# A four-layer network on one core: two of its statistics by accumulating ScalarE instructions, and a gate's factor by TensorE

## The chip, the core and the metric

The kernel runs on one core of a Trainium2 chip. A core has five engines with a queue each: TensorE (PE; its weight loads are listed apart as PEld), VectorE (DVE), ScalarE (ACT), GpSimd (POOL) and SyncE (SP, which here only issues DMAs). TensorE writes to PSUM alone, which has eight banks of 128 x 512 float32; VectorE and ScalarE read and write both PSUM and the working memory SBUF. The metric is the time of one execution in microseconds (us); the kernel is executed several times and the median is given.

## What is computed

The input is 16 images of 64 x 64 tokens with 256 channels, float32. There are four layers, each `x = x + layer(gn(x))`, where `gn` normalizes an image over 32 groups of 8 channels: the mean and the variance of a group are taken over all 4096 tokens and 8 channels.

```python
x = x + L0(gn(x))   # nearest of 1024 code vectors for each token
x = x + L1(gn(x))   # sigmoid attention along each image row
x = x + L2(gn(x))   # gate * gn(x), one gate per token
x = x + L3(gn(x))   # linear attention with 4 heads, then a layer norm
```

So four sets of statistics are needed per image: of the input, of layer 0's output, of layer 1's output and of layer 2's output. In layer 2 the gate of token n is a sigmoid of a softmax-weighted sum over all 4096 tokens. With gn(x) = (x - mean) * scale, and a mean that a later normalization takes out again, the output of layer 2 can be written per channel as (x - mean) * (1 + gate * scale); the kernel does that.

## The kernel before

The image is worked on with channels on the partitions: 256 channels are two blocks (index k) of 128, and 4096 tokens are 8 chunks (index ch) of 512. A chunk is a tile of 128 x 2 x 512 float32, 512 KB. Each layer is a Python generator per image that emits instructions for some chunks and then yields; a heap at the end of the program (`tasks`, `queue`, lines 891 to 921) interleaves the generators of different images by virtual start times and lengths (`LAG1`, `LEN1` and so on), in units of one image's search. In the steady state the search of image b (layer 0, `stage1`) is interleaved with layer 1 of image b-1 and the exponentials, the gate and layer 3 of earlier images. A scheduler then fixes one order per engine at compile time, by priority and by when it expects operands to be ready; `tc.high_priority` moves an instruction forward. On the chip each engine takes its queue in that order, and semaphores hold an instruction until its operands are there.

What the change touches:

- `chunk_stats` (line 255) issues one `bn_stats` on VectorE per chunk and block, which gives count, mean and variance of 512 elements. `gn_finish` (line 259) merges the eight chunks with `bn_aggr` and turns the per-channel numbers into `scale` and `-mean` per group, with small matmuls, ScalarE and GpSimd instructions.
- `back` (line 357, in `stage1`) finishes layer 0 for a chunk: TensorE transposes the tokens (input row plus code vector, added by a gathering DMA) to channels on partitions, into a PSUM bank `pt`; ScalarE copies `pt` to SBUF (line 364); VectorE takes statistics of that copy (line 257, tile `st_s<-xt_s`); the copy is stored.
- `stage2` (line 603) makes the exponentials (line 628, ScalarE) and their weighted sums (line 631, VectorE), and from them the gates, which it transposes to rows, copies and stores to memory as float32 (lines 649 to 652).
- `gate2` (line 664) loads a chunk of layer 1's output (`xg`), loads its 512 gates copied to all 128 partitions (`gb`, 256 KB written), and for each block: ScalarE makes `u = 1 + gate * scale` (line 685), VectorE makes `xg = (xg - mean) * u` (line 686) and takes statistics of it (line 257, tile `st_g<-xg_g`). The chunk goes to `out`, where layer 3 reads it.

PSUM is split into a pool of four banks (`ps_m`, the function `bank`), which nearly all stages share, and one of two double banks (`ps_w`, `wide`) for the search, `ph` and `po`. `put_row` (line 143) is the pattern that the change's new helper follows: a float32 row is cut into three bfloat16 parts whose sum gives it to about float32 precision, and a bfloat16 matmul against ones puts their sum on all partitions.

Of the kernel before, what the change touches and what calls it, by code (L numbers as in the profile page):

```python
# [16 lines left out]
P = 128  # L17
# [24 lines left out]
def kernel(  # L42
# [70 lines left out]
    PARTS = 3  # L113
    ones3 = const.tile([P, P], BF16, name="ones3")
# [5 lines left out]
    for n in range(PARTS - 1):  # L120
        nc.vector.tensor_scalar(
            below[:, n, n + 1 :], ident[0:PARTS, n + 1 : PARTS], -1.0, None, ALU.mult
        )

# [134 lines left out]
    def gn_finish(st, kind, b):  # L259

        tag = f"{kind}_{b}"
        mv = small.tile([P, NK, 2], F32, tag="gn_mv", name=f"mv_{tag}")
        for k in range(NK):
            nc.vector.bn_aggr(mv[:, k, :], st[:, k, :, :].rearrange("p c s -> p (c s)"))
        mean = mv[:, :, 0]
# [30 lines left out]
    def stats0(b):  # L296
# [8 lines left out]
        with tc.high_priority(offset=URGENT):  # L305
            norm0[b] = gn_finish(st, "n0", b)
# [5 lines left out]
    def stage1(b):  # L312
        tag = f"s1_{b}"
        scale, _, nbias = norm0.pop(b)
# [39 lines left out]
        st1 = stats_tile(1, f"st1_{tag}")  # L354
        x1_d[b] = []

        def back(ch):
            for k in range(NK):
# [5 lines left out]
                nc.scalar.copy(xt[ch][:, k, :], pt)  # L364
            chunk_stats(st1, xt[ch], ch)
# [51 lines left out]
        with tc.high_priority(offset=URGENT):  # L417
            norm1[b] = gn_finish(st1, "n1", b)
# [5 lines left out]
    def layer1(b):  # L424
# [118 lines left out]
        with tc.high_priority(offset=URGENT):  # L543
            norm2[b] = gn_finish(st2, "n2", b)
# [58 lines left out]
    def stage2(b, parts=1):  # L603
# [15 lines left out]
        gd = dram.tile([NT, P], F32, tag="gate", name=f"gd_{tag}")  # L619
        gates_d[b] = gd  # L620
        yield 2
        rest = gate2(b) if parts > 1 else None
        for part in range(parts):
# [26 lines left out]
            grow = small.tile([NT, P], F32, tag="grow", name=f"grow_{tag}_{part}", bufs=1)  # L650
            nc.scalar.copy(grow[:n, :], pg[:n, :P])
            nc.scalar.dma_start(out=gd[cols, :], in_=grow[:n, :])
# [11 lines left out]
    def gate2(b):  # L664
        tag = f"g2_{b}"
        scale, nmean, _ = norm2.pop(b)
        gd, x2 = gates_d.pop(b), x2_d.pop(b)
        st3 = stats_tile(3, f"st3_{tag}")
# [5 lines left out]
        for ch in range(NCHUNK):  # L674
            xt = xg.tile([P, NK, CW], F32, tag="xg", name=f"xg_{tag}_{ch}")
            nc.sync.dma_start(out=xt, in_=x2[ch])
            gb = s3p.tile([P, CW], F32, tag="gb", name=f"gb_{tag}_{ch}", bufs=2)
            nc.sync.dma_start(
                out=gb,
                in_=gd[ch * CH : (ch + 1) * CH, :].rearrange("t p -> (t p)").rearrange("(o n) -> o n", o=1)  # L680
                .to_broadcast([P, CW]),
            )
            for k in range(NK):
                u = s3p.tile([P, CW], F32, tag="u2", name=f"u_{tag}_{ch}_{k}")
                nc.scalar.activation(u, gb, AF.Identity, bias=one, scale=scale[:, k : k + 1])
                nc.vector.scalar_tensor_tensor(  # L686
                    xt[:, k, :], xt[:, k, :], nmean[:, k : k + 1], u, op0=ALU.add, op1=ALU.mult
                )
            chunk_stats(st3, xt, ch)
# [269 lines left out]
```

## Time and profile before

| | |
|---|---|
| median of 3 runs | 5701.88 us (5696.69 to 5706.75) |
| profiled execution | 5709.26 us; its span, first to last instruction, 5707.6 us |
| mean granted TensorE clock | 0.941 |
| busy: PE, DVE, ACT, POOL | 5070.7, 5046.3, 4578.7, 1929.1 us |
| `bn_stats` on DVE, line 257 | 4 x 256 instructions, 167.5 + 165.0 + 164.7 + 163.4 us |
| `u` on ACT, line 685 | 256 instructions, 199.4 us |
| copy of `pt` on ACT, line 364 | 256 instructions, 137.3 us |

In the groups of instructions a row gives line, engine, operation, the tiles out<-in, the shapes, the count; then busy time and mean duration of one; then the idle time of that engine just before them and what ended it. In the waits a row gives who waited for whom, the total, how often, and the longest. Durations of neighbours on an engine can overlap by some tens of nanoseconds, so that what one more instruction costs is better read from the distance between starts in the timeline.

### The profile page before, as it was taken

The page shows a single profiled execution, that of the slowest core. Times are in us where ns is not written, and L with a number is a line of the kernel's source. Part 1 is how long each engine was busy: PE and PEld are TensorE (multiplying, and loading weights), DVE is VectorE, ACT ScalarE, POOL GpSimd, SP SyncE. Part 2 cuts the span into 40 slices and gives each one's busy share as a digit, 9 for nine tenths or more (in the row PEclk, how much of TensorE's full clock was granted, in tenths as well). Part 3 has the DMA queues.
Part 4 walks back from the last instruction along what each step waited for, and adds up shares of the span by engine and source line. Part 5 has one row for each costly group of instructions (what it writes and reads, how often), then busy time and mean ns, then how long its engine had stood idle before and what let it go on. Part 6 is the DMA issues. An engine that isn't in the chain of part 4 may idle for free.

```text
span 5707.6 us, 71918 instructions
## 1 busy us (share of the span) xinstructions
PE 5070.7 (89%) x24911; PEld 2999.1 (53%) x24911; DVE 5046.3 (88%) x7186; ACT 4578.7 (80%) x6578; POOL 1929.1 (34%) x1203
## 2 busy tenths in 40 slices
PE   8978899889999999999989999899999999997777
PEld 3534455445555565554645555564555545564444
DVE  6489798999999999998999999999898998988982
ACT  4478587978889798887978888798887878888873
POOL 3123233323333334334333333333333333321332
PEclk9988999989999999999999999999999999997888
DMA  6453835655666757566575756757475674745544
GB/s 187 141 158 93 265 112 188 176 161 177 191 188 176 212 160 198 175 190 186 170 205 163 187 188 177 203 161 218 143 193 172 184 207 142 203 153 160 158 137 92
DMA packets 453763, 991.87 MB, mean 174 GB/s; under 512 B 50456, under 2 KB 198808, under 8 KB 445208
## 3 DMA queue, kind: packets, MB, share of 16 engines
q1 hardware_dynamic: 320272, 750.88, 39.7%
q0 software_dynamic: 92160, 134.26, 15.5%
q10 hardware_dynamic: 40968, 102.13, 4.6%
q8 instruction: 198, 3.24, 0.2%
q14 instruction: 165, 1.35, 0.1%
HBM read 684.07 MB, written 303.04 MB: 173 GB/s over the span
## 4 chain that ended last, share of the span: by engine, by line
PE 34%; DVE 19%; ACT 13%; issue 6%; POOL 3%; DMA 3%; ACTq 0%; SPq 0%; POOLq 0%; DVEq 0%
PE pd_s L386 11%; DVE ex_s L631 7%; ACT ex_s L628 6%; PE ph_l L476 3%; DVE i_s L397 3%; PE pqv_s L762 2%; PE pxo_s L874 2%; PE pk_s L745 2%; ACT nn_s L381 2%; DVE nn_s L392 2%; POOL qv_s L780 1%; PE po_l L516 1%; PE pz_s L835 1%; DVE st_s L257 1%; DVE xg_g L686 1%
## 5 line engine op out<-in xcount | busy, mean ns | idle before, releaser
L631 DVE CUSTOM_DVE_ANT_0 ex_s<-ex_s,x2b 128x2048 f32<-128x2048 f32 x1024 | 2364.2, 2315 | 77.0 <-ACT ex_s L628 75.1
L628 ACT ACTIVATE ex_s<-x0b,nmax_s,x_r 128x2048 f32<-128x2048 f32 x1024 | 2137.9, 2088 | 80.8 <-DVE num_s L631 77.8
L386 PE MATMUL pd_s<-e,xn_s 128*128 128x512 f32 x4096 | 2008.5, 625 | 71.6 <-DVE m L392 61.5
L398 POOL DMA_INDIRECT xc_s<-in_emb_rows,i_s x512 | 1160.6, 2267 | 1794.2 <-DVE i_s L397 1255.3
L386 PEld LDWEIGHTS pd_s<-e,xn_s 128*128 128x128 f32 x4096 | 763.4, 198 | 855.4 <-issue 705.3
L392 DVE CUSTOM_DVE_ANT_0 nn_s<-pd_s,nn_s 128x1024 f32<-128x1024 f32 x512 | 619.7, 1213 | 137.4 <-PE pd_s L386 100.5
L381 ACT ACTIVATE nn_s<-ne,nx_s 128x1024 f32<-128x1024 f32 x512 | 580.4, 1143 | 55.9 <-DVE nx_s L352 27.5
L397 DVE FIND_INDEX8 i_s<-m,nn_s 128x8 uint32<-128x1024 f32 x512 | 623.5, 1219 | 0.0
L476 PE MATMUL ph_l<-wh_l,xt_l 128*128 128x256 f32 x2048 | 536.1, 399 | 68.0 <-DVE xt_l L521 42.6
L762 PE MATMUL pqv_s<-wqv_s,xk_s 128*128 128x256 f32 x2048 | 488.7, 380 | 0.0
L476 PEld LDWEIGHTS ph_l<-wh_l,xt_l 128*128 128x128 f32 x2048 | 386.6, 196 | 193.1 <-issue 65.9
L762 PEld LDWEIGHTS pqv_s<-wqv_s,xk_s 128*128 128x128 f32 x2048 | 388.7, 191 | 120.2 <-issue 59.8
L780 POOL TENSOR_TENSOR qv_s<-qv_s,qm_s 128x512 f32<-128x512 f32 x128 | 216.1, 1688 | 640.0 <-DVE qm_s L779 329.3
L874 PE MATMUL pxo_s<-qo_s,wctx_s 128*128 128x512 f32 x512 | 279.5, 630 | 18.5 <-DVE qo_s L854 18.1
L736 POOL TENSOR_TENSOR qv_s<-qv_s,qd_s 128x512 f32<-128x512 f32 x128 | 186.1, 1454 | 324.7 <-DVE qd_s L735 189.8
L516 PE MATMUL po_l<-blk,h_l 128*128 128x128 f32 x2048 | 286.1, 291 | 3.6 <-DVE m L392 2.9
L516 PEld LDWEIGHTS po_l<-blk,h_l 128*128 128x128 f32 x2048 | 263.1, 202 | 42.2 <-issue 22.8
L884 POOL DMA_DIRECT2D out<-y_s x128 | 118.9, 929 | 479.3 <-ACT lrs_s L845 235.2
L745 PE MATMUL pk_s<-xk_s,wk_s 128*128 128x512 f32 x512 | 259.0, 626 | 0.0
L846 POOL TENSOR_TENSOR lrs_s<-lrs_s,mhalf 128x4 f32<-128x4 f32 x128 | 199.0, 1555 | 173.1 <-ACT lrs_s L845 164.2
L361 PE MATMUL pt_s<-ident,xc_s 128*128 128x128 f32 x1024 | 157.6, 289 | 103.6 <-DMA xc_s<-in_emb_rows,i_s 70.0
L875 ACT ACTIVATE y_s<-pxo_s,xm_g 128x512 f32<-128x512 f32 x256 | 174.6, 683 | 91.3 <-PE pxo_s L874 90.6
(191 smaller groups left out, 7012.6 us busy)
## 6 DMA issues: line engine op xcount, KB each, us to landing
xs_s<-in_xT SPq DMA_DIRECT2D x128, 512.0 KB
xt_s<-in_xT SPq DMA_DIRECT2D x128, 512.0 KB
xc_s<-in_x SPq DMA_DIRECT2D x128, 512.0 KB
x_s<-xt_s ACTq DMA_DIRECT2D x128, 512.0 KB
xt_l<-x_s SPq DMA_DIRECT2D x128, 512.0 KB
x_l<-xt_l SPq DMA_DIRECT2D x128, 512.0 KB
xr_r<-x_l SPq DMA_DIRECT2D x128, 512.0 KB
xg_g<-x_l SPq DMA_DIRECT2D x128, 512.0 KB
```

The lines of the kernel that those rows point to most:

```text
L381: nc.scalar.activation(nn, ne2, AF.Identity, bias=nx2[ch][:, t : t + 1])
L386: nc.tensor.matmul(pd[:, cols], lhsT=xn[ch][:, k, t * P : (t + 1) * P], rhs=e2[:, k, cols], start=(k == 0), stop=(k == NK - 1),)
L392: nc.vector.tensor_tensor_reduce(out=nn, in0=pd, in1=nn, scale=1.0, scalar=-3.0e38, op0=ALU.add, op1=ALU.max, accum_out=m8[:, 0:1],)
L397: nc.vector.max_index(i8, m8, nn)
L398: nc.gpsimd.indirect_dma_start(out=xc[ch][:, t, :], out_offset=None, in_=emb_rows, in_offset=bass.IndirectOffsetOnAxis(ap=i8[:, 0:1], axis=0),
L476: nc.tensor.matmul(ph[:, t, :], lhsT=X[:, k, t * P : (t + 1) * P], rhs=wh_n[:, k, :], start=(t % 2 == 0 and k == 0), stop=False, skip_grou ...
L516: nc.tensor.matmul(po[:, m : m + P], lhsT=h[:, t, k * P : (k + 1) * P], rhs=at[:, t, :, :].rearrange("p r i -> p (r i)"), start=True, stop ...
L628: nc.scalar.activation(ex, x0b, AF.Exp, bias=nmax[:, T : T + 1], scale=x01[:, T, 1:2], accum_out=den[:, h, T : T + 1])
L631: nc.vector.tensor_tensor_reduce(out=ex, in0=ex, in1=x2b, scale=1.0, scalar=0.0, op0=ALU.mult, op1=ALU.add, accum_out=num[:, h, T : T + 1],)
L745: nc.tensor.matmul(pk, lhsT=wk_n[:, k, :], rhs=xt[:, k, :], start=(k == 0), stop=(k == NK - 1))
L762: nc.tensor.matmul(pqv[:, j, :], lhsT=xt[:, k, t * P : (t + 1) * P], rhs=wqv_n[:, k, :], start=(j == 0 and k == 0), stop=False, skip_group ...
L874: nc.tensor.matmul(px, lhsT=wctx[:, 1, pr * P : (pr + 1) * P], rhs=qT, start=True, stop=True)
```

## The change

Statistics of layer 0's output: the copies of line 364 become `activation(Copy)` with an accumulator output (the sum over 512 tokens), and a second ScalarE instruction squares `pt` in place, shifted by the group mean of the input, with an accumulator (the sum of squares). `bn_stats` on these chunks is gone.

The gated residual: the gates are stored as three bfloat16 parts. A chunk's gates are loaded to 3 x 3 partitions by three DMAs in place of one that filled 128. The scale is cut into three bfloat16 parts once per image by `put_scale`. One bfloat16 matmul per block of 9 products plus a row of ones gives `u` in a PSUM bank. VectorE's product reads `u` there and has an accumulator; ScalarE squares the result into the same bank with an accumulator. `bn_stats` on these chunks is gone too. `aggregate_sums` turns the sums of both places into mean and variance per channel.

```diff
+    def put_scale(dst, scale, tag):
+        v = small.tile([P, NK, GP + 1], F32, tag="v10", name=f"v10_{tag}", bufs=1)
+        nc.gpsimd.memset(v, 0.0)
+        nc.scalar.copy(v[:, :, 0:GP], scale.unsqueeze(2).to_broadcast([P, NK, GP]))
+        pb = bank(f"psr_{tag}")
+        row = pb[: GP + 1, :C]
+        for k in range(NK):
+            nc.tensor.matmul(row[:, k * P : (k + 1) * P], lhsT=v[:, k, :], rhs=ident, ...)
+        for n in range(PARTS - 1):
+            top = small.tile([GP + 1, C], BF16, tag="stop", name=f"stop_{tag}_{n}", bufs=1)
+            nc.scalar.copy(top, row)
+            nc.tensor.matmul(row, lhsT=below_s[:, n, :], rhs=top, start=False, stop=True, ...)
+        nc.scalar.activation(dst[0 : GP + 1, :], row, AF.Identity, bias=ident[0 : GP + 1, GP : GP + 1])
...
+    def aggregate_sums(st, shift, tag):
+        mv = small.tile([P, NK, 2], F32, tag="gn_mv", name=f"mv_{tag}")
+        nc.vector.tensor_reduce(mv, st.rearrange("p c k s -> p k s c"), AX.X, ALU.add)
+        nc.vector.tensor_scalar(mv, mv, 1.0 / TOK, None, ALU.mult)
+        dev = small.tile([P, NK], F32, tag="gn_dev", name=f"dev_{tag}", bufs=1)
+        if shift is None:
+            nc.vector.tensor_tensor(dev, mv[:, :, 0], mv[:, :, 0], ALU.mult)
+        else:
+            nc.vector.tensor_tensor(dev, mv[:, :, 0], shift, ALU.add)
+            nc.vector.tensor_tensor(dev, dev, dev, ALU.mult)
+        nc.vector.tensor_tensor(mv[:, :, 1], mv[:, :, 1], dev, ALU.subtract)
+        return mv
...
-                nc.scalar.copy(xt[ch][:, k, :], pt)
-            chunk_stats(st1, xt[ch], ch)
+                nc.scalar.activation(xt[ch][:, k, :], pt, AF.Copy, accum_out=st1[:, ch, k, 0:1])
+                nc.scalar.activation(
+                    pt, pt, AF.Square, bias=shift[:, k : k + 1], accum_out=st1[:, ch, k, 1:2]
+                )
...
-            norm1[b] = gn_finish(st1, "n1", b)
+            norm1[b] = gn_finish(aggregate_sums(st1, shift, f"n1_{b}"), "n1", b)
...
-        gd = dram.tile([NT, P], F32, tag="gate", name=f"gd_{tag}")
+        gd = dram.tile([PARTS, NT, P], BF16, tag="gate", name=f"gd_{tag}")
         gates_d[b] = gd
+        put_scale(scale_rows[b % 2], norm2[b][0], tag)
...
-            nc.scalar.copy(grow[:n, :], pg[:n, :P])
-            nc.scalar.dma_start(out=gd[cols, :], in_=grow[:n, :])
+            nc.scalar.copy(grow[:n, 0, :], pg[:n, :P])
+            nc.vector.tensor_tensor(left[:n, :], pg[:n, :P], grow[:n, 0, :], ALU.subtract)
+            nc.vector.tensor_copy(grow[:n, 1, :], left[:n, :])
+            nc.vector.tensor_tensor(grow[:n, 2, :], left[:n, :], grow[:n, 1, :], ALU.subtract)
+            nc.scalar.dma_start(out=gd[:, cols, :].rearrange("i t p -> t i p"), in_=grow[:n, :, :])
...
-            gb = s3p.tile([P, CW], F32, tag="gb", name=f"gb_{tag}_{ch}", bufs=2)
-            nc.sync.dma_start(out=gb, in_=gd[ch * CH : (ch + 1) * CH, :]...to_broadcast([P, CW]))
+            gr = gate_rows[ch % 2]
+            for i in range(PARTS):
+                nc.sync.dma_start(
+                    out=gr[PARTS * i : PARTS * (i + 1), :],
+                    in_=gd[i : i + 1, ch * CH : (ch + 1) * CH, :]...to_broadcast([PARTS, CW]),
+                )
             for k in range(NK):
-                u = s3p.tile([P, CW], F32, tag="u2", name=f"u_{tag}_{ch}_{k}")
-                nc.scalar.activation(u, gb, AF.Identity, bias=one, scale=scale[:, k : k + 1])
+                u = bank(f"pu_{tag}_{ch}_{k}")
+                nc.tensor.matmul(u, lhsT=srow[:, k * P : (k + 1) * P], rhs=gr, start=True, stop=True)
                 nc.vector.scalar_tensor_tensor(
-                    xt[:, k, :], xt[:, k, :], nmean[:, k : k + 1], u, op0=ALU.add, op1=ALU.mult
-                )
-            chunk_stats(st3, xt, ch)
+                    xt[:, k, :], xt[:, k, :], nmean[:, k : k + 1], u, op0=ALU.add, op1=ALU.mult,
+                    accum_out=st3[:, ch, k, 0:1],
+                )
+                nc.scalar.activation(u, xt[:, k, :], AF.Square, accum_out=st3[:, ch, k, 1:2])
...
-            scale, nmean, _ = gn_finish(st3, "n3", b)
+            scale, nmean, _ = gn_finish(aggregate_sums(st3, None, f"n3_{b}"), "n3", b)
```

The statistics of the input and of layer 1's output stay with `bn_stats` and `bn_aggr`, which `aggregate` now holds. `gate_rows` and `scale_rows` are constant tiles of 128 partitions, two of each, whose rows past the tenth stay zero.

## Prediction

> **What bounds the kernel now.** First the page's totals, then a stretch of seven images in the steady state (from the start of image 6's search to that of image 13's), since filling and draining have other limits.
>
> ```profile
> PE 5070.7 (89%) x24911; PEld 2999.1 (53%) x24911; DVE 5046.3 (88%) x7186; ACT 4578.7 (80%) x6578; POOL 1929.1 (34%) x1203
> ```
> ```profile
> core 0: us, PE busy (x) PEld busy (x) DVE busy (x) ACT busy (x) POOL busy (x), PEclk, DMA share, GB/s
> 2011.00:4361.00 2350.00, 2157.06 (x10844) 1287.70 (x10843) 2182.65 (x3104) 1988.68 (x2858) 863.08 (x517) 0.96 0.64 184
> 0.00:1017.00 1017.00, 882.47 (x4113) 475.65 (x4114) 806.92 (x1194) 693.01 (x959) 304.42 (x195) 0.93 0.55 164
> 5036.00:5708.00 672.00, 513.43 (x2402) 338.70 (x2402) 506.40 (x708) 488.11 (x756) 165.81 (x137) 0.86 0.49 139
> ```
>
> Divided by seven, one image takes 335.7 us: VectorE busy 311.8 (idle 23.9), ScalarE 284.1 (idle 51.6), TensorE 308.1. The last is flattering: matmul durations overlap. Counting from start to next start, with each interval capped at its line's median, I get 266 us of TensorE per image. So VectorE is nearest to full, with ScalarE 28 us behind. The chain that ended last agrees that no engine rules alone (PE 34%, DVE 19%, ACT 13% of the span): the three hand work to each other in fixed orders, and waits at the hand-overs make up the rest. The waits of the same seven images:
>
> ```profile
> ACT qv_s L781 <- POOL qv_s L780: 85.6, 45, 6.7
> ACT ex_s L628 <- DVE num_s L631: 44.1, 25, 2.7
> DVE ex_s L631 <- ACT ex_s L628: 37.7, 23, 3.9
> PE pt_s L361 <- ACT qv_s L767: 12.9, 7, 1.9
> ACT al_s L752 <- DVE nkm_s L751: 11.3, 9, 2.3
> ```
>
> ScalarE waits for VectorE's exponential sums 6.3 us per image, for GpSimd 12.2, the rest for many small matmul results; VectorE waits for ScalarE's exponentials 5.4.
>
> **Prices.** Groups over the whole run, then the timeline of ScalarE and of VectorE, for what one more instruction really takes.
>
> ```profile
> L257 DVE BATCH_NORM_STATS2 st_g<-xg_g 128x6 f32<-128x512 f32 x256 | 165.0, 681 | 0.1
> L257 DVE BATCH_NORM_STATS2 st_s<-xt_s 128x6 f32<-128x512 f32 x256 | 164.7, 682 | 21.0 <-ACT xt_s L364 20.9
> L875 ACT ACTIVATE y_s<-pxo_s,xm_g 128x512 f32<-128x512 f32 x256 | 174.6, 683 | 91.3 <-PE pxo_s L874 90.6
> L781 ACT ACTIVATE qv_s<-qv_s 128x512 f32<-128x512 f32 x128 | 80.5, 629 | 174.2 <-POOL qv_s L780 173.6
> ```
> ```profile
> 3405.67 0.67 ACT L754 ACTIVATE kx_s<-pk_s,nkm_s 128x512 f32<-128x512 f32 x1
> 3406.24 0.19 ACT L754 ACTIVATION_READ_ACCUMULATOR kx_s<-pk_s,nkm_s 128x1 f32 x1
> 3406.33 1.51 ACT L685 ACTIVATE u_g<-gb_g,one,s_n 128x512 f32<-128x512 f32 x2
> 3407.74 2.09 ACT L628 ACTIVATE ex_s<-x0b,nmax_s,x_r 128x2048 f32<-128x2048 f32 x1
> ```
> ```profile
> 3411.49 1.28 DVE L257 BATCH_NORM_STATS2 st_g<-xg_g 128x6 f32<-128x512 f32 x2
> 3412.69 2.28 DVE L631 CUSTOM_DVE_ANT_0 ex_s<-ex_s,x2b 128x2048 f32<-128x2048 f32 x1
> ```
>
> Start to start, a `bn_stats` takes 0.60 (1.20 for two); a PSUM activation with a pointer bias 0.57; the accumulator's read 0.09, though its row says 0.19; one `u` 0.70.
>
> **VectorE, per image.** Removed: 32 `bn_stats` x 0.60 = 19.2, and four `bn_aggr` (row mean 0.33, 0.23 start to start) = 0.9. Added: accumulator reads on 16 products, 16 x 0.08 (row of `num_s`) = 1.3; `u` now from PSUM: the nearest rows are the products with a PSUM operand, 0.341 at 128 and 0.480 at 256 elements, so by their slope about 0.76 at 512 against a median of 0.75 now: 0, between -1 (the mean now is 0.81) and +1; nine tiny operations of `aggregate_sums` about 0.1 each = 0.9; three for the gate's parts = 0.4. Net **-17.5**: 311.8 becomes 294.
>
> **ScalarE, per image.** Layer 0: 16 squares (0.57 + 0.09) = 10.6, 16 reads behind the copies = 1.5. Gate: 16 x `u` at 0.70 gives way to 16 squares without pointers, nearest L781, 0.63 less the 0.10 of overlap = 0.53, plus 0.09: -1.3. `put_scale`: a copy at 0.09 and three casts at 0.25 (starts of `put_row`'s) = 0.9. Net **+11.7**: 284.1 becomes 296. The page "ScalarE: Activation LUTs" of the Trainium skill (Rules for kernel authors) speaks against this: adds and multiplies belong on VectorE, which it calls up to three times as fast per element, for bfloat16. Here data is float32 and the rows give 0.66 against 0.60, so moving a statistic costs a tenth, not threefold; by the rule's factor ScalarE would gain 29 us instead of 12 and the change would lose about 15 per image. I take the rows.
>
> **TensorE.** 16 bfloat16 matmuls of 512 columns; the nearest, L481, has a row of 0.388 but 0.215 start to start: 3.4, and 0.5 for `put_scale`. 266 becomes 270; hidden in its idle 66. Without that cover, 3.9.
>
> **DMAs.** 128 gate loads of 256 KB become 384 of 3 KB: 33 MB of 992 less to move, and nothing now waits for that bandwidth (64% busy). SP issues two more per chunk, 0.32 each (its row at the end of the run); loads queued behind them come 0.64 later, and they have two to four buffers: 0, or 5 us per image if not. GpSimd gets one memset per image; the copy behind it can be held by a gather, whose row is 2.27: 0 to 3, I take 1. The store of the gates now waits on ScalarE's queue for three VectorE operations, once per image: 0 to 4, I take 1.
>
> **New waits.** (1) A square of the gated chunk stands in ScalarE's queue behind VectorE's product; behind it stand exponentials and the copies that free PSUM. Nearest: `al_s` behind `nkm_s`, 11.3 us over 49 events, 0.23 each; x16 = 3.7. If all waited as long as those that did, 1.26: 20. If the schedule always puts other work between: 0. I take 4. (2) PSUM. `pt` is held one square longer, and `u` goes through three engines. From first matmul to last reader, the bank most like `u` (`pk`: TensorE, VectorE, ScalarE) is held 7.8 us, and all of the four banks' tenants together 540 of 1344 bank-us per image. Sixteen `u` and longer `pt` add 145: 40% becomes 51%. "PSUM — Partial Sum Buffer" (summary of rules) says to evacuate promptly, as PSUM is tight; the trace so far shows little of it: `pt` waited seven times for a bank in seven images, 1.9 each. By the rule, with each of the 32 affected tenants stalling TensorE once, 59 us, within TensorE's spare 66 but passed on as late results; by the row, two or three more stalls, 5 us, hidden. I take 0 on the end and 59 as the far end of the range. (3) The chain of tiny VectorE operations before `gn_finish` is longer, and 2.3-us sums can slip between: up to 10 us later for layer 1 and layer 3 of that image, which start tens of us later anyway (search of image 9 ends at 3682, its layer 1 starts at 3723): 0.
>
> **The sum.** ScalarE, at 296, becomes the fullest. What idles beside it? The present leader idles 23.9, ScalarE now 51.6. As ScalarE runs later, results it waits for are more often ready, and its 6.3 for VectorE shrinks, against (1), put_scale and the store, 6 together. I take the middle, 37.7: **333.5 per image**, 2.2 less. Over the twelve steady images (1017 to 5036) -27; head and tail, where the engines idle more, the same 0.7% of 1689, -11 (the last gates' chain: a smaller load saves about 2 of 5 to 6 us twice, three more operations take about 1 each time). Profiled 5709.3 - 38 = 5671; the profiled execution lies 7 above the median shown, so against that: **5664**.
>
> **Rivals.** (a) VectorE's relief pays in full: ScalarE idles only the leader's 24, 296 + 24 = 320 per image, 12 x 15.7 + 30 = 218 less: 5485. For it: a leading engine now shows 24. Against it: two engines within 2 us of each other, where there were 28 between. (b) Nothing measurable: the total of the three engines stays (862 to 860), so the hand-overs, not the fullest engine, set the pace: 335 to 336, 5690 to 5713. (c) Slower: ScalarE keeps its waits. Its queue already stops for GpSimd, TensorE and VectorE, and a square behind a product is one stop more. The point that decides is 335.7 - 296 = 40 us of idle per image: above it the kernel is slower. At 45.3 (now, without the wait for sums) plus 3.7, less what a fuller queue absorbs (a few), about 46: 342 per image, 12 x 6.3 = 76, 5778.
>
> **How the numbers follow.** The likeliest 0.40, (a) 0.12, (b) 0.09, (c) 0.39. A difference under 0.2% (11 us) is what a measurement of this kernel can't tell from none. Faster 0.52, same 0.09, slower 0.39. The likeliest's own range is 5590 to 5690; to hold 8 in 10 I go from 5570 (part of (a)) to 5800 ((c) with its waits at 48).
>
> **What would show it.** Over a steady stretch of seven images: VectorE about 294 and ScalarE about 296 busy per image; 16 more squares with a row near 0.68 in `pt`, 16 near 0.63 on the gated chunk; `u` gone from ScalarE. Right if ScalarE's idle falls under 40 per image. Wrong toward slower if the waits show squares or copies held by the product, or TensorE held for banks by squares; wrong toward faster if ScalarE idles under 30. A row of the PSUM product over 0.9, or accumulator reads that cost their full 0.19, would break the prices.

## The result: slower by 0.9 %

The changed kernel takes 5752.51 us (median of 4 runs, 5749.96 to 5757.46) against 5704.32 (4 runs, 5696.69 to 5707.21): a ratio of 1.0088, 95 % interval 1.0072 to 1.0104. The forecast was 5664, so its sign was wrong; its range, 5570 to 5800, holds the result. Rival (c), the slower one, had 5778.

The page's totals of the changed kernel:

```profile
PE 5122.0 (89%) x25256; PEld 3010.9 (52%) x25263; DVE 4757.6 (83%) x7081; ACT 4735.6 (82%) x7666; POOL 1969.4 (34%) x1226
```

VectorE lost 289 us of work (5046 to 4758) and ScalarE gained 157 (4579 to 4736); the span went from 5707.6 to 5748.2. By stage, the windows of the same seven images, of the head and of the tail (window, length, then busy time and instructions of each engine, granted clock, DMA share, GB/s):

```profile
core 0: us, PE busy (x) PEld busy (x) DVE busy (x) ACT busy (x) POOL busy (x), PEclk, DMA share, GB/s
2007.70:4394.10 2386.40, 2186.51 (x11043) 1296.72 (x11042) 2061.17 (x3062) 2058.14 (x3340) 879.07 (x526) 0.96 0.61 176
0.00:1004.00 1004.00, 872.32 (x4092) 470.24 (x4096) 758.36 (x1144) 728.29 (x1153) 300.07 (x202) 0.93 0.55 163
5061.20:5748.20 687.00, 537.82 (x2512) 352.37 (x2512) 489.86 (x761) 497.99 (x841) 175.20 (x140) 0.87 0.46 131
```

Images are counted from 0; the seven run from the start of image 7's search to that of image 14's, and so does the stretch that the prediction calls images 6 to 13. One image takes 2386.4 / 7 = 340.9 us. VectorE is busy for 294.5 of them (idle 46.4), ScalarE for 294.0 (idle 46.9). The clock is the same 0.96 as before. From the start of image 4's search (1006.2 before, 1004.0 after) to the end of the last one (5023.3 and 5061.2) the steady part grew by 40 us; the head is 2 shorter and the tail 3 longer, so the loss sits in the steady images.

The prices, from the groups of instructions of the whole run, each shape apart (busy time, mean ns of one, then the idle time ahead and what ended it), and from ScalarE's timeline:

```profile
L418 ACT ACTIVATE pt_s<-pt_s,nm_n 128x512 f32<-128x512 f32 x256 | 166.8, 652 | 0.0
L751 ACT ACTIVATE pu_g<-xg_g 128x512 f32<-128x512 f32 x256 | 150.5, 588 | 19.4 <-DVE xg_g L747 15.5 <-issue 1.3 <-ACT ex_s L684 0.9
L747 DVE SCALAR_TENSOR_TENSOR xg_g<-xg_g,nm_n,pu_g 128x512 f32<-128x512 f32 x256 | 182.8, 740 | 18.7 <-PE pu_g L746 13.5 <-DMA xg_g<-x_l 5.0
L746 PE MATMUL pu_g<-gate_rows,scale_rows 128*128 128x512 bf16 x249 | 81.8, 391 | 21.9 <-DMA gate_rows<-gd_s 13.3 <-ACT qv_s L829 6.2 <-DVE qo_s L916 1.0
L551 PE MATMUL psc_l<-fg_l 32*64 32x64 f32 x2048 | 71.0, 230 | 7.5 <-ACT pt_s L418 2.4 <-ACT qv_s L829 2.2 <-ACT pu_g L751 2.0
```
```profile
3654.36 0.19 ACT L417 ACTIVATION_READ_ACCUMULATOR xt_s<-pt_s 128x1 f32 x1
3654.45 0.62 ACT L418 ACTIVATE pt_s<-pt_s,nm_n 128x512 f32<-128x512 f32 x1
3655.02 0.18 ACT L418 ACTIVATION_READ_ACCUMULATOR pt_s<-pt_s,nm_n 128x1 f32 x1
```

Start to start a square takes 0.57 and an accumulator read 0.09, as the working had it. The square of the gated chunk waited for VectorE's product only 15.5 us in the whole run, 1.0 per image. A PSUM bank held by a new square cost TensorE little: at the scores of layer 1 (the last row) 2.4 + 2.0 us in the whole run.

Where the waiting went, from the waits of the seven images (who waited for whom: total, how often, longest):

```profile
DVE ex_s L687 <- ACT ex_s L684: 114.3, 44, 12.0
ACT qv_s L843 <- POOL qv_s L842: 96.8, 38, 9.0
ACT top_qv_s L190 <- PE prow_qv_s L197: 46.6, 7, 8.6
PE pt_s L414 <- DMA xc_s<-in_emb_rows,i_s: 36.6, 8, 6.6
DVE gate_s L701 <- ACT gate_s L700: 36.6, 6, 8.2
PE pg_n L321 <- DVE mv_n L305: 36.4, 7, 6.9
```

ScalarE's wait for VectorE's sums (44.1 before) is gone from the list, as forecast. In its place stand few, long stops: the last four rows come six to eight times in seven images, 4.6 to 6.7 us each in the mean, and the longest of all is 12.0. Three places hold most of them: the transposes that wait for a **gather** (until 286 us into the image; with it stand ScalarE's cast `top_qv_s` behind TensorE's `prow_qv_s`, and VectorE's sum), the **gate** (until 330 us), and the **norm** `pg_n` (until 24 us). Idle stretches over 3.5 us, summed from the trace over ten images, are per image 1.6 us of TensorE, 5.8 of VectorE and 5.9 of ScalarE before, and 13.5, 13.6 and 13.0 after.

Two things keep these sums in proportion. ScalarE's long stops at `qv_s`, by the gate, were there before (5.1 us per image, 5.2 after); what is new for ScalarE is the gather's (none before, 6.5 after), and TensorE didn't stand at the gate before (0, now 3.4). And TensorE's idle time in all, by the two windows, went only from 27.6 to 28.6 per image: the long stops took the place of many short waits, so their length can't be counted as loss. (By its rows TensorE's busy time rose by 4.2 per image. That the added matmuls alone pace the kernel is ruled out below: the gate's part alone has the same ones and is faster.)

The same loss by place in the image: the distance between the index searches on VectorE of the last tile of one chunk and of the next, median of images 9 to 14, in us.

| chunk | 0 | 1 | 2 | 3 | 4 | 5 | 6 | 7 |
|---|---|---|---|---|---|---|---|---|
| before | 52.5 | 53.7 | 33.3 | 47.2 | 49.8 | 39.8 | 33.7 | 29.1 |
| after | 57.8 | 55.7 | 31.9 | 42.9 | 43.3 | 37.1 | 41.4 | 32.3 |

Chunks 2 to 5 gain 15 us (170.1 to 155.2), chunks 6, 7, 0 and 1 lose 18 (169.0 to 187.2).

### The profile page after: what moved, and what is told of

Read it like the earlier page. It is cut to its first block, busy times and chain, and to the rows that moved or that the text cites. A ratio compares the mean times of both kernels' runs of the same rounds, so it can differ in the third digit from the quotient of the medians.

```text
span 5748.2 us, 74108 instructions
## 1 busy us (share of the span) xinstructions
PE 5122.0 (89%) x25256; PEld 3010.9 (52%) x25263; DVE 4757.6 (83%) x7081; ACT 4735.6 (82%) x7666; POOL 1969.4 (34%) x1226
## 5 line engine op out<-in xcount | busy, mean ns | idle before, releaser
L453 POOL DMA_INDIRECT xc_s<-in_emb_rows,i_s x512 | 1128.9, 2205 | 1728.2 <-DVE i_s L452 1086.1
L531 PE MATMUL ph_l<-wh_l,xt_l 128*128 128x256 f32 x2048 | 513.3, 387 | 10.1 <-DVE xt_l L576 7.0
L842 POOL TENSOR_TENSOR qv_s<-qv_s,qm_s 128x512 f32<-128x512 f32 x128 | 240.7, 1880 | 712.6 <-DVE qm_s L841 575.8
L908 POOL TENSOR_TENSOR lrs_s<-lrs_s,mhalf 128x4 f32<-128x4 f32 x128 | 239.1, 1868 | 159.8 <-ACT lrs_s L907 152.0
L807 PE MATMUL pk_s<-xk_s,wk_s 128*128 128x512 f32 x512 | 271.8, 657 | 0.0
L798 POOL TENSOR_TENSOR qv_s<-qv_s,qd_s 128x512 f32<-128x512 f32 x128 | 174.2, 1361 | 236.3 <-DVE qd_s L797 196.9
```

Source lines behind the costliest of these rows:

```text
L453: nc.gpsimd.indirect_dma_start(out=xc[ch][:, t, :], out_offset=None, in_=emb_rows, in_offset=bass.IndirectOffsetOnAxis(ap=i8[:, 0:1], axis=0),
L531: nc.tensor.matmul(ph[:, t, :], lhsT=X[:, k, t * P : (t + 1) * P], rhs=wh_n[:, k, :], start=(t % 2 == 0 and k == 0), stop=False, skip_grou ...
L807: nc.tensor.matmul(pk, lhsT=wk_n[:, k, :], rhs=xt[:, k, :], start=(k == 0), stop=(k == NK - 1))
```

## The experiments

The expectations number their theories: 1, the loss is two stops per image, at layer 3's weight row behind a gather and at the gate; 2, ScalarE sets the pace and keeps its waits; 3, a loop of waits through the weight row; 4, it matters where in the image ScalarE's work lies; 5, the order moves the time anywhere; 6, a meeting on GpSimd's queue.

Each row: ratio to the kernel before, run beside it on the same chip, with its 95 % interval; then, from the trace of one execution of each kernel, means over ten images: the distance of two images, busy time of VectorE and ScalarE, ScalarE's idle time, and TensorE's stops over 3.5 us. All in us per image.

| kernel | time | ratio | image | DVE | ACT | ACT idle | PE stops |
|---|---|---|---|---|---|---|---|
| before | 5704.3 | 1 | 336.0 | 312.2 | 284.3 | 51.7 | 1.6 |
| after | 5752.5 | 1.0088 (1.0072 to 1.0104) | 341.2 | 294.9 | 294.0 | 47.2 | 13.5 |
| layer 0's part alone | 5731.2 | 1.0053 (1.0036 to 1.0070) | 339.3 | 303.8 | 295.7 | 43.6 | 4.7 |
| gate's part alone | 5675.5 | 0.9956 (0.9935 to 0.9978) | 333.1 | 304.0 | 283.2 | 49.9 | 4.9 |
| only `u` by TensorE | 5739.5 | 1.0067 (1.0044 to 1.0089) | 335.2 | 314.6 | 274.9 | 60.3 | 1.2 |
| after, input's statistics earlier | 5691.4 | 0.9960 (0.9941 to 0.9979) | 334.9 | 295.2 | 295.2 | 39.7 | 7.8 |
| before, the same | 5683.2 | 0.9954 (0.9933 to 0.9974) | 333.3 | 312.6 | 284.0 | 49.3 | 1.8 |
| after, later | 5757.4 | 1.0116 (1.0083 to 1.0148) | 341.1 | 294.7 | 294.6 | 46.5 | 12.0 |
| before, later | 5683.1 | 0.9967 (0.9948 to 0.9986) | 333.8 | 312.2 | 284.2 | 49.6 | 0.7 |
| after, norm at common priority | 5741.9 | 1.0053 (1.0034 to 1.0073) | 340.4 | 294.8 | 294.7 | 45.8 | 9.2 |
| before, the same | 5706.3 | 1.0003 (0.9984 to 1.0022) | 335.6 | 312.3 | 284.1 | 51.4 | 2.4 |
| gate's part, row and statistics moved | 5616.9 | 0.9847 (0.9820 to 0.9874) | 329.7 | 304.0 | 283.5 | 46.2 | 4.7 |

### The parts of the change

Layer 0's part alone keeps the diff of `back` and of `norm1`; the gate's part alone keeps the rest. The third takes `u` from TensorE and leaves the statistics of the gated chunk with `bn_stats`:

```diff
                     xt[:, k, :], xt[:, k, :], nmean[:, k : k + 1], u, op0=ALU.add, op1=ALU.mult,
-                    accum_out=st3[:, ch, k, 0:1],
                 )
-                nc.scalar.activation(u, xt[:, k, :], AF.Square, accum_out=st3[:, ch, k, 1:2])
+            chunk_stats(st3, xt, ch)
```

> Only the statistics of layer 0's output move to ScalarE; the gate stays as before. Busy per steady image by the rows: ScalarE 284 to 296, VectorE 312 to 302. Theory 1 (the loss is two stops per image in which all engines stand, one at layer 3's row of weights behind a gather, one at the gate's exponential behind GpSimd): no fixed sign, within 25 us of before, and slower only if the trace shows one of the two stops. Theory 2 (ScalarE paces the kernel and keeps its waits of 45 to 50 us per image whatever the load): 343 per image, so some 5790 us, 85 slower than before.

> Only the gate's part: u by TensorE, sums by VectorE's product and ScalarE's squares; layer 0's statistics stay with bn_stats. Busy per steady image: ScalarE 284 as before, VectorE 312 to 304. Theory 1: faster only if neither stop appears; within 25 us of before otherwise. Theory 2: ScalarE no fuller, VectorE 8 us emptier, so 328 to 334 per image, 20 to 90 us faster than before (5610 to 5680).

> Only the gate's factor by TensorE; bn_stats stays for both statistics, and ScalarE neither makes u nor squares. Busy per steady image: ScalarE 284 to 273, VectorE 312. Theory 2 (about half a microsecond of the period per microsecond of ScalarE, 0.3 per microsecond of VectorE, as the two runs of one part each gave): 5 to 6 us less per image, 5625 to 5645. If VectorE alone paced the kernel: no gain, 5690 to 5715.

The two halves have opposite signs: +30 us for layer 0's part, -26 for the gate's. Their sum is +4, the whole change is +48: there is something that only both together bring. That the half which adds ScalarE work (11.4 per image) loses, and the half which adds none gains, is what theory 2 (ScalarE sets the pace) wants, though it forecast 85 us for layer 0's part. The third run contradicts it as a full account: with ScalarE 9 us emptier per image it is 0.7 % slower, and only 0.8 us per image faster in the steady part; the rest goes in head and tail (15 us longer up to the start of image 5's search, 19 from that of image 15's). Why isn't settled.

### The all-reduce on GpSimd, and layer 3's weight row

At the stop by the gate GpSimd stands still before its all-reduce over partitions and again after it. Both kernels were run with the all-reduce replaced by a transpose, a maximum and a small matmul:

```diff
-        nc.gpsimd.partition_all_reduce(ab, ext, P, bass_isa.ReduceOp.max)
+        nc.tensor.transpose(pe[:2, :P], ext, ident)
+        nc.vector.tensor_reduce(top2, pe[:2, :P], AX.X, ALU.max)
+        nc.vector.tensor_scalar(dg, ident[0:2, 0:2], top2, None, ALU.mult)
+        nc.tensor.matmul(pa[:, 0:2], lhsT=ones2, rhs=dg, start=True, stop=True)
+        nc.vector.tensor_copy(ab, pa[:, 0:2])
```

> The changed kernel with the maximum over partitions taken by a TensorE transpose, a VectorE maximum and a small matmul in place of GpSimd's partition_all_reduce, so that GpSimd isn't stopped before and after it (about 8 and 10 us per image). Theory 1: the stop at the gate's exponential (ScalarE 6 us, VectorE 5 us, TensorE 4 us per image) goes, 60 to 110 us less than the changed kernel, 5640 to 5690. Theory 2: ScalarE's load is the same and its waits spread elsewhere; 5720 to 5750.

> The same replacement in the kernel before. There ScalarE stands 5.3 us and VectorE 3.5 us per image at GpSimd's stop. Theory 1: 40 to 60 us less than before, 5640 to 5665, so that both kernels end within 25 us of each other. Theory 2: the kernel before gains less than 30 us, or both gain the same and the changed one stays 40 to 50 us above.

Measured: 5755.2 (1.0096, 1.0072 to 1.0119) for the changed kernel and 5769.0 (1.0122, 1.0096 to 1.0148) for the one before. The stop at the gate is gone in both, and neither is faster; the kernel before has no stop over 3.5 us left on VectorE and is 1.2 % slower. A long stop is not a loss by itself.

The second remedy takes the weight row whose casts waited (`put_row` in layer 3) out of the raised priority, in the changed kernel, the one before, and the gate's part alone:

```diff
-            put_row(qv_row, nmean, by_weight(wqv_n), f"qv_{tag}")
+        put_row(qv_row, nmean, by_weight(wqv_n), f"qv_{tag}")
```

> The changed kernel, with layer 3's row of weights (put_row in stage3) moved out of the raised priority, so that on TensorE it comes behind the transposes and the next search tiles instead of between two transposes. Nothing else is edited. Theory 3 (ScalarE runs late in the changed kernel, the search's code index is late, and the fixed order then closes a loop: ScalarE's cast waits for TensorE's row, which stands behind transposes that wait for a gather, which waits for VectorE's index, which waits for ScalarE): the loop's 6.5 us of ScalarE and some 7 us of VectorE per image go, 330 to 336 per image, 60 to 120 us less than the changed kernel, 5635 to 5690. Theory 2 (ScalarE's waits persist and move elsewhere): within 25 us of the changed kernel, 5730 to 5775.

> The same edit in the kernel before, where the loop costs ScalarE 2 us per image. Theory 3: 0 to 25 us less than before. Theory 2: within 15 us of before.

> Only the gate's part of the change (as in the earlier run of the gate alone, 26 us faster than before), with the same edit of the row of weights. Theory 3: the loop didn't show in that run, so -20 to +10 us against it, 5655 to 5685. Theory 2: the same within 10 us.

5754.6 (1.0102, 1.0063 to 1.0141), 5703.6 (1.0006, 0.9991 to 1.0021) and 5663.3 (0.9933, 0.9914 to 0.9952). In the changed kernel TensorE still stops 6.2 us per image for the gather; only the ScalarE instruction that waits behind it is another, the copy of `pt`. So the row was not the cause of that stop, the gather was.

### Is it where in the image ScalarE works? No

Theory 4 took the table by chunks at its word: the relief pays where the engines are full (chunks 2 to 5), the added ScalarE work costs at the image boundary. It can be split there, with ScalarE's sums for half of layer 0's chunks (`SQUARED`: 1 to 4, or 0, 5, 6 and 7) and `bn_stats` for the others:

```diff
+                if ch in SQUARED:
                     nc.scalar.activation(xt[ch][:, k, :], pt, AF.Copy, accum_out=sums[...])
                     nc.scalar.activation(pt, pt, AF.Square, bias=shift[:, k : k + 1], accum_out=sums[...])
+                else:
+                    nc.scalar.copy(xt[ch][:, k, :], pt)
+            if ch not in SQUARED:
+                chunk_stats(st1, xt[ch], ...)
```

> The changed kernel, but layer 0's statistics come from ScalarE's sums only for the chunks 1 to 4 of an image (whose copies fall into chunks 2 to 5 of the search, where all three engines are nearly full) and from bn_stats for the chunks 0, 5, 6 and 7; the two halves are merged by three more tiny VectorE operations. Theory 4 (VectorE's relief pays where engines are full, and ScalarE's added work costs at the image boundary, where hand-overs set the pace): chunks 2 to 5 take about 156 us as in the changed kernel, the other four about 172 as with the gate's part alone, sum about 327 per image, 5560 to 5620. Theory 2 (ScalarE's whole load sets the pace): half way between the gate's part alone (5675) and the changed kernel (5752), 5705 to 5725. Theory 5 (what the fixed order happens to line up, anywhere): no relation, 5660 to 5780.

> The opposite half: ScalarE's sums for the chunks 0, 5, 6 and 7 of layer 0, bn_stats for 1 to 4. Theory 4: chunks 2 to 5 as with the gate's part alone, 165 us, the boundary as in the changed kernel, 186: 350 per image, 5800 to 5870, the slowest of all. Theory 2: as the other half, 5705 to 5725. Theory 5: no relation, 5660 to 5780.

> As the run with ScalarE's sums for the chunks 1 to 4 alone, and layer 3's weight row without its raised priority. The row's move gave 12 us with the gate's part alone, 1 before the change and -2 in the changed kernel. Theory 4: as the former, less up to 12: 5550 to 5620. Theory 2: 5700 to 5725. Theory 5: no relation to the former run, apart by 10 to 50 us.

The middle half took 5757.7 (1.0072, 1.0051 to 1.0093), the edges 5717.6 (1.0007, 0.9993 to 1.0020), the middle with the row later 5768.3 (1.0085, 1.0053 to 1.0117). Theory 4 forecast the order the other way round and falls. The middle half gained in chunks 2 to 5 as forecast (156.1 us) but then lost 13.5 us in chunk 0, where from image 9 on a tile of the search waits 7.9 us for VectorE, 24 us into the image. A gain in one part of the image was given back in another, so gains by chunk can't be added up.

### The meeting on GpSimd's queue

What stands in front of the late gather? GpSimd's timeline of the changed kernel at that place in image 11, then VectorE's, then TensorE's (start, duration, instruction; in brackets the idle time before and what ended it):

```profile
3633.69 0.72 POOL L332 TENSOR_TENSOR s_n<-s_n,mhalf 128x2 f32<-128x2 f32 x1 [7.24 <-ACT s_n L329]
3634.49 1.77 POOL L334 TENSOR_TENSOR nb_n<-nm_n,s_n 128x2 f32<-128x2 f32 x1
3636.22 2.82 POOL L332 TENSOR_TENSOR s_n<-s_n,mhalf 128x2 f32<-128x2 f32 x1
3639.12 0.20 POOL L334 TENSOR_TENSOR nb_n<-nm_n,s_n 128x2 f32<-128x2 f32 x1
3639.96 1.62 POOL L453 DMA_INDIRECT xc_s<-in_emb_rows,i_s  x1 [0.65 <-issue]
```
```profile
3632.80 1.21 DVE L452 FIND_INDEX8 i_s<-m,nn_s 128x8 uint32<-128x1024 f32 x1
3633.94 2.27 DVE L687 CUSTOM_DVE_ANT_0 ex_s<-ex_s,x2b 128x2048 f32<-128x2048 f32 x1
3636.21 2.28 DVE L687 CUSTOM_DVE_ANT_0 ex_s<-ex_s,x2b 128x2048 f32<-128x2048 f32 x1
```
```profile
3648.84 0.69 PE L414 MATMUL pt_s<-ident,xc_s 128*128 128x128 f32 x2 [6.15 <-DMA xc_s<-in_emb_rows,i_s]
```

The same place in the kernel before, in image 10, GpSimd and then VectorE:

```profile
3277.89 0.19 POOL L281 TENSOR_TENSOR nb_n<-nm_n,s_n 128x2 f32<-128x2 f32 x1
3278.80 3.21 POOL L398 DMA_INDIRECT xc_s<-in_emb_rows,i_s  x1 [0.72 <-DVE i_s L397]
```
```profile
3277.11 1.22 DVE L397 FIND_INDEX8 i_s<-m,nn_s 128x8 uint32<-128x1024 f32 x1
```

There the norms are done just before the index (3277.11 + 1.22 = 3278.33), and the gather follows it by 0.47. In the changed kernel the index of tile 23 (the last of chunk 5) is there at 3632.80 + 1.21 = 3634.01. The gather that needs it is issued at 3639.96, since two group norms (two powers and two products: of the input of a coming image, and of layer 1's output for the gate) stand ahead of it on GpSimd's queue. It lands just before 3648.84, where TensorE has waited 6.15 us. Four GpSimd operations on 128 x 2 elements took 5.6 us, though the same forms take 0.72 and 0.20 elsewhere. The two long ones end 0.05 and 0.55 us after the rows of VectorE's sums beside them (3636.21 and 3638.49): that is taken up below.

Over ten images the gather of tile 23 follows its index by a median of 0.7 us before (2.4 in four of the ten, behind the last product of a norm), 5.9 after, 2.4 with layer 0's part alone, 0.5 with the gate's part alone. Of these four only the whole change has the meeting in full, which fits an excess that only both parts together bring. Theory 6: this meeting is the loss. It is tested by starting the statistics of the input (and so that norm) a tenth of an image earlier, in both kernels (and, further down, a tenth later, with `b - 0.6`); theory 5 says that any such shift of the order moves the time:

```diff
-            tasks.append((b - 0.7, 0.5, stats0(b), 14))
+            tasks.append((b - 0.8, 0.5, stats0(b), 14))
```

> The changed kernel, with the statistics of a coming image's input begun a tenth of an image earlier, so that their group norm (n0) no longer falls together with the gate's (n2) and the two chains on GpSimd do not stand ahead of the search's gathers together. If those chains hold the gather that the transposes wait for: the yearly stop before the transposes (6.6 us longest) falls under 3 and the time to about 5710, since chunk 6 of the search (41.4 us against 33.7) comes back by some 4 us per image. If the gather is late because ScalarE and VectorE ahead of it are late: the stop stays, 5745 to 5760. If nothing but the placement of work by the order matters: either way by 10 to 40 us.

> The kernel before, with the statistics of a coming image's input begun a tenth of an image earlier: the control to the same edit in the changed kernel, which gained 61 us there. In the kernel before, the two norms of that place stand 6 us apart on GpSimd, and the gather of the search's tile 23 follows its index by 0.7 us, against 5.9 in the changed kernel. Theory 6 (the change let the two norms meet in front of that gather, and the 6 us per image are the loss): nothing to gain here, 5695 to 5715. Theory 5 (any shift of the order moves the time, and the gain was luck): away from 5704 by 20 to 60 us, either way. If the kernel before gains the same 1.3 %: 5630 to 5645, and the shift says nothing on the change.

(The "yearly stop" of the first text is the stop that comes once per image.) The changed kernel comes to 0.9960: relative to itself -1.3 %. GpSimd and TensorE at that place in this run:

```profile
3602.43 0.73 POOL L332 TENSOR_TENSOR s_n<-s_n,mhalf 128x2 f32<-128x2 f32 x1 [3.44 <-ACT s_n L329]
3603.24 0.19 POOL L334 TENSOR_TENSOR nb_n<-nm_n,s_n 128x2 f32<-128x2 f32 x1
3604.09 3.23 POOL L453 DMA_INDIRECT xc_s<-in_emb_rows,i_s  x1 [0.66 <-DVE i_s L452]
```
```profile
3610.24 0.71 PE L414 MATMUL pt_s<-ident,xc_s 128*128 128x128 f32 x5
```

One norm, the gather 0.5 us behind its index, and transposes that wait for nothing. Chunk 6 of the search takes 34.5 us in place of 41.4. But the control gains too, to 0.9954, against the forecast of no change. So a shift by itself is worth 0.46 % (half-width 0.2) in a kernel whose gather is hardly prompter for it (mean delay 1.3 us unshifted, 1.1 shifted), and the change, at this placement, costs 0.9960 / 0.9954 = 1.0006, with an interval of about 0.28 % each way (the two half-widths, 0.19 and 0.21, added in squares). Of the loss of 0.88 %, about 0.8 % goes with the shift, and the difference to the control is not to be told from none.

> The changed kernel, with those statistics begun a tenth of an image later than now, so that the norms are pulled apart in the other direction. Theory 6: the gather of tile 23 follows its index by under 1.5 us, the stop before the transposes goes, and 4 to 6 us per image come back: 5680 to 5705, unless the norm then falls into GpSimd's stop for the all-reduce and the next search starts late. Theory 5: no relation to the gather's delay, 5690 to 5790.

> The kernel before with those statistics begun a tenth later. Theory 6: the gather isn't held in the kernel before, so nothing to gain, 5695 to 5720, or slower by the next search's start if the norm falls into GpSimd's stop. Theory 5: away by 20 to 60 us, either way. Together with the same shift in the other direction it shows how far a shift of the order alone moves a kernel in which nothing collides.

The other direction brings the changed kernel nothing (1.0116, 5757 against the 5680 to 5705 of theory 6), the one before again 0.3 % (0.9967, against its forecast of nothing). The gather of tile 23 is prompt here (0.5 us), as forecast, and yet nothing is won. GpSimd and ScalarE in that run show why:

```profile
3642.83 3.19 POOL L453 DMA_INDIRECT xc_s<-in_emb_rows,i_s  x1 [8.48 <-DVE i_s L452]
3645.41 2.02 POOL L332 TENSOR_TENSOR s_n<-s_n,mhalf 128x2 f32<-128x2 f32 x1
```
```profile
3647.47 0.50 ACT L612 ACTIVATE wrow_n<-wrow_raw,s_n 128x12 f32<-128x12 f32 x2 [3.83 <-POOL s_n L332]
```

Now the gather stands first, and the gate's norm, whose operand came at 3641.55, is served at 3645.41 and done at 3647.43. ScalarE waits 3.8 us for it, with the search's `nn_s` behind it, and TensorE 4.8. Whichever of the two comes first, the other is late by 4 to 6 us, and all three busy engines stop for it.

A second way to part them leaves the task's start alone and takes the raised priority from the norm of the input:

```diff
-        with tc.high_priority(offset=URGENT):
-            norm0[b] = gn_finish(aggregate(st, f"n0_{b}"), "n0", b)
+        norm0[b] = gn_finish(aggregate(st, f"n0_{b}"), "n0", b)
```

> The changed kernel, with the group norm of the input (n0) at common priority in place of the raised one: a second way, without moving a task, to keep it from standing with the gate's norm in front of the gather of tile 23. Theory 6, as it stands after the shifts (on GpSimd's queue a norm and a gather that come due together make one of them 4 to 6 us late, and the full engines wait): if tile 23's gather follows its index by under 1.5 us and no norm waits behind a gather, 5690 to 5720; if they meet in another way, 5740 to 5770. Theory 5 (the order moves the time without regard to that queue): no relation to the longest stops of TensorE.

> The same edit in the kernel before, as the control. Both shifts of the norm gained it about 20 us. Theory 6: TensorE's stops over 3.5 us stay under 5 us per image, 5680 to 5710, so that the changed kernel's gain, if it has one, is larger by some 40. Theory 5: no relation between the two, 5660 to 5760.

1.0053 and 1.0003: a third of a per cent for the changed kernel, nothing for the one before. In images 9 to 14 the gather is prompt, but again stands ahead of both norms (the power took 2.02 us there); in images 5 to 8 it is late as before by 2.5 to 5.9. This is the branch "if they meet in another way", just inside its lower end.

So at four placements of one norm the change costs 0.9, 0.1, 1.5 and 0.5 % against the control of the same placement (intervals of 0.2 to 0.4 each way). It costs nothing that can be measured where norm and gather keep apart, and 0.5 to 1.5 where they meet. It gains clear of noise in none.

Two further pairs fit. With the all-reduce replaced the gather of tile 23 follows its index by 0.5 us (median) in both kernels, without any shift, and the change costs 1.0096 / 1.0122 = 0.9974 (about 0.35 % each way): nothing that can be measured, though neither kernel is fast. With the weight row moved the gather stays 5.9 us late, and the change costs 1.0102 / 1.0006 = 1.0096 (about 0.4 each way).

What these pairs don't separate is the stop at the gate. TensorE stands there 3.7 us per image in the changed kernel, counting every wait over 0.1 us; 4.0, 3.1 and 5.5 with the norm later, at common priority, and with the row later; 2.6 with the norm earlier; 0 with the all-reduce replaced, and 0 in every kernel without the change. So it is long where the change costs, too. That the early placement keeps most of it and costs nothing speaks for the meeting, but no run removes the one and keeps the other. Nor does either explain every loss: ScalarE's sums for the middle half lose 0.7 % with a gather delayed 0.5 us, and `u` alone loses as much with the same 0.5 and no stop at the gate.

The shift was also put on the fastest variant, the gate's part alone with the row later:

> The fastest so far (the gate's part alone with layer 3's weight row at common priority, 5663) with the statistics of the input begun a tenth earlier. There the gather of tile 23 follows its index by 0.5 us already. Theory 6: nothing to gain, 5650 to 5675. Theory 5: away by 20 to 60 us.

5616.9, 1.5 % faster than the kernel before (0.9847, 0.9820 to 0.9874) and the fastest of all. Theory 6 alone had no gain here and is 33 us short; theory 5 is right in so far as this shift moves every kernel, by 0.5 to 1.3 %. This variant also has TensorE waiting 7.8 us for `pg_n` in six of ten images, longer than in the changed kernel (6.9): that stop, the third of the list above, is not what the change lost by.

## Why the prediction was wrong, point by point

**Right: the work.** VectorE at 294 per image measured 294.5; ScalarE at 296 measured 294.0; squares at rows of 0.652 and 0.588 us (near 0.68 and near 0.63 taken); the product from PSUM at 0.740 (0.75); `u` on TensorE at 0.391 (0.388). The DMAs moved 960 MB in place of 992. The rule weighed for ScalarE (the Trainium skill, "ScalarE: Activation LUTs", Rules for kernel authors) would have had ScalarE gain 29 us per image: it gained 9.9, near the 11.7 of the rows.

**Right: the new waits (1) and (2) are small.** A square behind a product costs 1.0 per image (4 taken), waits for banks next to nothing. The far end of 59 us, an estimate from the rule of "PSUM — Partial Sum Buffer" (summary of rules) to evacuate promptly, was not seen.

**Wrong: "What idles beside it? ... I take the middle, 37.7".** This is the step that failed. Measured in the window of seven images it was 46.9, and the sum shows what that is worth: 294.0 + 46.9 = 340.9, where 335.7 - 294.0 = 41.7 would have been even. The argument for the middle was that a later ScalarE finds more of its operands ready. That was so for VectorE's sums (44.1 us in seven images to nothing), but other waits took their place, and they came as few long stops. With norm and gather apart, ScalarE idles 39.7 per image, close to the middle that was taken, and the image takes 334.9 (333.5 forecast). The control at that placement, though, takes 333.3: even there the sum's gain isn't found, and that 39.7 comes close to 37.7 there may be luck. The forecast missed its 37.7 mostly by what the shift removes, the meeting first of all, and its gain by more than that.

**Wrong: GpSimd at "0 to 3, I take 1".** The working costed the one instruction that the change adds to GpSimd's queue, not how the instructions that were there already would stand to each other once VectorE and ScalarE ran at another pace. The gather's median delay grew from 0.7 to 5.9 us though the change added none of the four instructions that now stand between its index and it. As far as the pairs of runs show, this is the mechanism behind the failed step; the stop at the gate isn't excluded beside it.

**Not shown wrong: (3), the longer chain ahead of the norms, 0.** TensorE's wait for `pg_n` did grow, from 19.4 to 36.4 us in seven images (longest 4.5 to 6.9), but not by that chain: with the gate's part alone this norm keeps its `bn_aggr`, and the longest waits are 7.4 to 7.6. The wait costs nothing visible in the total: the fastest variant has the longest of these waits.

**Wrong: head and tail, -11.** Measured about +1.

**The rivals.** (c) had the side, the break-even of 40 and nearly the idle time (46). Its reason, that ScalarE keeps its waits and gets one stop more behind a product, is not what happened: those waits did go. (b), that the sum of the three engines stays and so nothing is won, is what the experiments leave at the placements without the meeting (1.0006 and 0.9974). An argument that fits it, which isn't shown: from the two halves alone, a microsecond of VectorE's work is worth 0.29 of the image's time and one of ScalarE's 0.50 (-8.4 and +11.4 gave +3.3; -8.2 and -1.1 gave -2.9). Then -17.3 and +9.7 come to -0.1: the trade is even. These weights give +0.6 for the earlier placement (1.6 measured) and -2.7 for the gate's part there (-3.6, with the row moved), but -4.0 for `u` alone, where -0.8 was measured. They give -0.1 for the whole change at its own placement too, where 5.2 was measured.

**Open.** Why every shift of the input's statistics gains 0.3 to 0.5 % in the kernel before; why taking `u` from ScalarE alone loses in head and tail; why layer 0's part costs 30 us alone, where the gather is held 2.4 us only. Moving the norms off GpSimd, which would remove the meeting and leave the rest of the order nearly as it is, was not tried; nor was anything that removes the stop at the gate alone.

## What to carry to other kernels

In a kernel whose three main engines are each over 80 % busy in a fixed order, a change of the pace is also a change of who meets whom in the small queue beside them: list, for each rare instruction on that queue, what stands within a few microseconds of it and which full engine waits for it, and cost a meeting (here an instruction late by 4 to 6 us, once per image) beside the work that is moved. Before such a change is judged, run it and the old kernel at two or three placements of a neighbouring task: here one and the same change measured +1.5 to +0.1 %, and a shift of 0.1 in a start time moved the old kernel by 0.5. Split a change and measure its parts: one half of this one was worth keeping, and with the order moved it made the fastest kernel.

## What the runs showed of the hardware

**GpSimd stands still while VectorE runs the weighted sum with two SBUF inputs.** The product of a norm (128 x 2 elements, line 334) takes 0.19 us. In the changed kernel 13 of 64 started while such a sum ran; their median is 1.78 us, and they end 0.05 to 0.06 us after the sum's row. The other 51 never take over 0.20. Of the powers, the 36 that met none take 0.72 (at most 0.74); of the other 28, 15 are held, for up to 2.84, and end 0.55 to 0.60 us after the sum's row. Gathers take 1.56 us (median of 183 without such a sum beside them, at most 1.85) and 3.3 (median of 263 with over 1 us of it). The page "SBUF — State Buffer" of the Trainium skill (SBUF: two separate sides) states the mechanism: VectorE and GpSimd share a pair of ports under an exclusive lock, which a VectorE instruction with two SBUF inputs takes for its whole length against a GpSimd operation that reads SBUF. The trace agrees. With 1024 sums of 2.3 us, 2353 of 5748 us, GpSimd at 34 % busy is less free than it looks, and its durations in a profile contain VectorE's. The prediction read the gather's 2.27 as a price; it is a mean over both kinds, with medians of 1.56 and 3.32 in that kernel.

**The all-reduce brings stops of its own:**

```profile
3675.96 1.81 POOL L667 PARTITION_ALL_REDUCE ab_s<-ext_s  x1 [5.96 <-DVE i_s L452]
3692.27 1.04 POOL L842 TENSOR_TENSOR qv_s<-qv_s,qm_s 128x512 f32<-128x512 f32 x1 [10.79 <-issue]
```

Behind a row of 1.8 us, and one gather more, GpSimd is idle 10.8 us before the next product, with nothing in the profile that it waits for. The trace has a `MODIFY_POOL_CONFIG` on its queue at 3669.7, 6.3 us ahead of the all-reduce, and another at 3681.0, 11.3 us ahead of that product. ScalarE's waits of up to 9.0 us for `qv_s` are in that gap. Taking the all-reduce away removed these stops and made neither kernel faster.
